# A sandwich block kernel: the chains of the third and fourth batch item are taken with up to two steps in a slot

## The chip, the cores and the metric

The kernel runs on one core of a Trainium2 chip. The metric is the device time of one execution in microseconds (us); lower is better. Each kernel is run several times and the median is given, and one further execution is taken with the hardware profiler on. Engine names in the profile: PE is TensorE (matmuls), PEld its weight loads, DVE is VectorE, ACT is ScalarE, POOL is GpSimd, SP is SyncE, which in this kernel only issues DMAs.

## The reference

The input x has 16 batch items of 512 tokens with 128 features. Two layers, each with a layernorm before it, a layernorm on its output and a residual, are applied:

```
u  = layernorm(x)
Bu = u @ B_w.T                        # 64 states
h  = causal convolution of Bu with exp(t * log(eig))   # by FFT, real part
y  = h @ C_w.T + D * u
x  = x + layernorm(y)

n  = layernorm(x)
p  = softmax(n @ w_router) * softmax(n @ w_gating / 0.1)   # 8 experts
cw = p / (sum(p) + 1e-9)
f  = sum over experts e of cw[e] * ((silu(n @ w_gate[e]) * (n @ w_up[e])) @ w_down[e])
x  = x + layernorm(f)
```

Every expert (128 to 512 to 128) is computed for every token, so the matmuls of the experts are nearly all of the work.

## The kernel before

**Blocks and slots.** A block b is one batch item: 512 tokens, held as 128 features x 512 tokens for the matmuls. The main loop (`for n in range(total + LAG)`, line 804) runs over slots: a slot n is one quarter (128 of 512 hidden units) of one expert of one block, so a block has 32 slots and the loop 512. In a slot `up(n)` issues six matmuls of 128x512 (gate g and up projection uu, each as three products of split fp32 parts, line 337 to 339), and `down(n - 4)` three more (d). A weight or activation is split into a high part, rounded to fp32r, and a low part that holds the rest. ScalarE takes silu of g (`sg`, line 563), VectorE multiplies it with uu (`gate`, line 574), ScalarE rounds the product to `hi` (line 579), and VectorE or POOL computes `lo` (line 585). g has two banks of PSUM and uu three, so g(n+2) needs silu(n) done, and uu(n+3) needs the reader of uu(n) done. Every engine takes its instructions in the order in which the program issues them, and so does SP's DMA queue: an instruction that waits holds up all behind it on its engine.

**After an expert.** In the first slot after its last `down` has been issued and two more have passed (slot 32b + 9, then every fourth slot), `combine` multiplies the expert's output by the token weights `cwb` on VectorE (line 600 for the first expert of a block, 605 for others) and POOL adds (line 608). When a block is done, `back(b)` transposes it through DRAM (`ob`, four `sco` writes, one `ot` read, lines 472 to 480), normalises it and stores it.

**Chains.** What a block needs ahead of its experts is a generator, `chain(b)`: `front(b)` (line 345) and `route(b)` (line 407). front: statistics of xt, its layernorm u, u transposed to features, split into uh and ul, the product bu (three matmuls), times a table (v), a running sum (scan, line 380), times the table, the product yp, plus du, a layernorm, the residual x2, a layernorm xn, xn transposed, split into xh and xl. Blocks 0, 1 and 15 are transposed on TensorE; the others go through DRAM in `features`: a transpose within 32x32 squares on VectorE (`blk_u` or `blk_x`, line 324), four writes `scr` (line 327), and one read `ft` (line 332) that waits on SP until the writes have landed. route: logits on TensorE (line 414), eight exponentials on POOL (line 432, 1.64 us each), normalisation on VectorE, then `cwT`, four small writes `scw` (line 453), and four reads `cwb` (line 461) of 512 KB each, which spread the weights of two experts over all partitions; three buffers hold them.

**The planner.** Chains are cut into steps. A generator yields ahead of each step `delay, DVE, ACT, POOL` (and "f" when the step takes the single bank ps_f): how many slots after the step before it may come at the earliest, and what the step is thought to cost each engine. `busy` holds what is issued on the three engines and not worked off at 1.94 us a slot; `take` refuses a step that would go over. For every chain in order of its rank (block number, and b + 0.5 for `back(b)`), `steps(n)` (line 791) takes up to `1 + hurry` steps in slot n, and shortens each delay by `hurry` unless the step takes ps_f:

```
for _ in range(1 + hurry):
    if n >= x[0] and not (own[0] and x[1][3:]) and take(x[1][:3]):
        ...
        x[0], x[1] = n + (y[0] if y[4:] else max(y[0] - hurry, 0)), y[1:]
```

`begin(n, rank, g, hurry=0)` (line 786) enters a chain: block 0's route and block 1's chain at slot 0 with hurry 1, every later chain at slot max(4, 32 b - 67) with hurry 0, so block 2 at slot 4, block 3 at slot 29 and block 4 at slot 61. Block 2's experts begin at slot 64 and block 3's at 96. Two delays are counted from the slot at hand: `max(1, 32 * b - 8 - now[0])` ahead of cwT, and `max(1, 32 * b + 8 * i + 2 - now[0])` ahead of each cwb. Which engine computes lo (`lo_pool[n]`, line 842) follows from `busy` too: POOL when it has less to do than VectorE.

**Early slots.** Through slot 26 the weights of the experts are split as well (`split_w`, line 113): ScalarE and POOL each have one 128x512 operation for it in three slots of four, and SP loads five ahead.

Of the kernel before, what the change touches and what calls it, by code (L numbers as in the profile page):

```python
# [47 lines left out]
def sandwich(ctx, tc, x, a_params, B_w, C_w, Dv, w_router, w_gating, w_gate, w_up, w_down, sines, out):  # L48
# [417 lines left out]
    def back(b, acc):  # L466

        x2 = blocks[b]["x2"]
        yield 2, 0.6, 0, 0
        ob = work(f"ob{b}").rearrange("p (q c i) -> p q c i", q=4, c=NT)  # L470
        order = "p (c q i) -> p q c i" if on_pe(b) else "p (q c i) -> p q c i"
        vec.transpose(ob, acc.rearrange(order, q=4, c=NT))
        scr = dram.tile([4, 32, 4, P], F32, name=f"sco{b}", tag="sco")
        for j in range(4):
            nc.sync.dma_start(
                out=scr[:, :, j].rearrange("q i m -> i q m"),
                in_=ob[32 * j : 32 * j + 32].rearrange("p q c k -> p q (c k)"),
            )
        ot = work(f"ot{b}").rearrange("p (j c k) -> p j c k", j=4, c=NT)
        nc.sync.dma_start(out=ot.rearrange("p j c k -> p (j c k)"), in_=scr.rearrange("q i j m -> (q i) (j m)"))  # L480
        views = [ot[:, :, c] for c in range(NT)]
        rs, nm = yield from ln_coef(views, 6)
        if "x2m" in blocks[b]:
            vec.tensor_tensor(nm, nm, blocks[b]["x2m"], ALU.add)
        jk = x2.rearrange("p c (j k) -> p c j k", j=4)
        yield from ln_add(gp, jk, ot.rearrange("p j c k -> p c j k"), views, views, jk, rs, nm)
        nc.sync.dma_start(out=out[b].rearrange("(c p) d -> p c d", p=P), in_=x2)
# [65 lines left out]
    def up(n, between=lambda: None):  # L553
        b, e, fc = n // 32, n // 4 % 8, n % 4
        B = blocks[b]
        cs = slice(128 * fc, 128 * fc + 128)
        g = ps_g.tile([P, T], F32, name=f"g{n}", tag="g")
        mm3(g, W[0, e], cs, B["xh"], B["xl"], True, True)
        between()
        u = ps_u.tile([P, T], F32, name=f"uu{n}", tag="u")  # L560
        mm3(u, W[1, e], cs, B["xh"], B["xl"], True, True)
        s = hp.tile([P, T], F32, name=f"sg{n}", tag="sg", bufs=2)
        act.activation(s, g, AF.Silu)  # L563
        pend[n] = s, u
# [3 lines left out]
    def gate(n):  # L568
        s, u = pend[n]
        if lo_pool[n]:  # L570
            h = hp.tile([P, T], F32, name=f"hh{n}", tag="hh", bufs=2)
        else:
            h = u
        vec.tensor_tensor(h, s, u, ALU.mult)  # L574
        pend[n] = h

    def split_hi(n):
        hi = hp.tile([P, T], F32R, name=f"hi{n}", tag="hi", bufs=LAG + 1)
        act.copy(hi, pend[n])  # L579
        pend[n] = pend[n], hi  # L580

    def split_lo(n):
        h, hi = pend[n]
        lo = hp.tile([P, T], F32R, name=f"lo{n}", tag="lo", bufs=LAG + 1)
        (gp if lo_pool[n] else vec).tensor_tensor(lo, h, hi.bitcast(F32), ALU.subtract)  # L585
        pend[n] = hi, lo

    def down(n):
        b, e, fc = n // 32, n // 4 % 8, n % 4
        if fc == 0:  # L590
            dps[b, e] = ps_d.tile([P, T], F32, name=f"d{n}", tag="d")
        cs = slice(128 * fc, 128 * fc + 128)
        mm3(dps[b, e], W[2, e], cs, *pend.pop(n), fc == 0, fc == NF - 1)

    def combine(b, e):
        ps = dps.pop((b, e))
        cw = blocks[b]["cwb"][e // 2][:, e % 2]
        if e == 0:
            accs[b] = fe.tile([P, T], F32, name=f"acc{b}", tag="acc")
            vec.tensor_tensor(accs[b], ps, cw, ALU.mult)  # L600
        elif b == NB - 1 and e == E - 1:
            finish(b, accs.pop(b), ps, cw)
        else:
            t = hp.tile([P, T], F32, name=f"ct{b}_{e}", tag="ct", bufs=2)
            vec.tensor_tensor(t, ps, cw, ALU.mult)  # L605
            eng = vec if (b, e) >= (NB - 1, E - 3) else gp
            acc = accs[b]
            add = lambda: eng.tensor_tensor(acc, acc, t, ALU.add)  # L608
            if (b, e) == (NB - 1, E - 2):
                late.append(add)  # L610
            else:
                add()

    def chain(b):
        yield from front(b)
        yield from route(b)
# [4 lines left out]
    def split_next(k):  # L621
        nonlocal nsplit
        for _ in range(k):
            if nsplit < 3 * E:
                split_w(nsplit)
                nsplit += 1
# [151 lines left out]
    def take(need, most=(0.9, 0.8, 2.0)):  # L778

        if any(c and busy[i] + c > SLOT + most[i] for i, c in enumerate(need)):  # L780
            return False
        for i, c in enumerate(need):
            busy[i] += c
        return True

    def begin(n, rank, g, hurry=0, head=None):
        d, *need = head or next(g)
        side.append([n + d, need, g, hurry, rank])
        side.sort(key=lambda x: x[4])

    def steps(n):
        for x in list(side):
            hurry = x[3]
            for _ in range(1 + hurry):
                if n >= x[0] and not (own[0] and x[1][3:]) and take(x[1][:3]):
                    own[0] = own[0] or bool(x[1][3:])
                    y = next(x[2], None)
                    if y is None:
                        side.remove(x)
                        break  # L800
                    x[0], x[1] = n + (y[0] if y[4:] else max(y[0] - hurry, 0)), y[1:]

    own[0] = False
    for n in range(total + LAG):
        b, s = divmod(n, 32)
        now[0] = n
        busy = [max(0.0, t - SLOT) for t in busy]
        if n < total:
            take((0.6, 1.0, 0), (9, 9, 9))
        if 0 <= n - 1 < total:  # L810
            take((0, 0, 1.23) if lo_pool[n - 1] else (0.6, 0, 0), (9, 9, 9))
            split_hi(n - 1)
        if n < total:
            up(n, *[first] * (n == 0))
        if n == 0:
            begin(n, 0, first_route, 1, routed)
            if NB > 1:
                begin(n, 1, chain(1), 1)
        if n == 3:
            act.copy(bT[0], bT32)  # L820
            gp.tensor_tensor(bT[1], bT32, bT[0].bitcast(F32), ALU.subtract)
        for i in range(NB):
            if i > 1 and n == max(4, 32 * i - LEAD):
                begin(n, i, chain(i))
        m = n - LAG
        if 0 <= m < total:
            down(m)
        m = n - LAG - (2 if n < total else n == total)
        if m >= 0 and m % 4 == 3:
            take((0.6, 0, 1.23), (9, 9, 9))  # L830
            combine(m // 32, m // 4 % 8)
            if m % 32 == 31 and m // 32 in accs:
                begin(n, m // 32 + 0.5, back(m // 32, accs.pop(m // 32)))
        if nsplit < 3 * E and n < total and n % 4 < 3:
            take((0, 0.5, 1.23), (9, 9, 9))
            split_next(1)
        if n < total:
            steps(n)
        if 0 <= n - 1 < total:
            split_lo(n - 1)  # L840
        if n < total:
            lo_pool[n] = busy[2] < busy[0] and n < total - 3
            gate(n)
# [27 lines left out]
```

## Time and profile before

| | us |
|---|---|
| median of 3 runs (lowest, highest) | 1145.75 (1145.21, 1145.89) |
| the profiled execution | 1146.53 |
| its span, first to last instruction | 1144.7 |
| TensorE busy | 1121.9 |
| VectorE, ScalarE, POOL busy | 870.9, 710.3, 764.9 |
| DMA, mean over the span | 62 GB/s |

Where TensorE is idle, by stretches of 20 us (20 less its busy time there): 7.2 in 0 to 20, 3.0 in 20 to 40, 0.6 in 40 to 60, 1.5 in 60 to 80, 0.3 in 80 to 100, 0.4 in 120 to 140, 2.8 in 180 to 200, and 2.2 in 1120 to 1140; in all others it is 0. A busy matmul is counted for about 0.39 us while the next one starts 0.229 us after it, so busy time tells only where TensorE waits; how long is read from the starts.

Slot times, as the start of g(n) in the trace: slot 4 at 33.87, 8 at 44.46, 13 at 55.57, 19 at 69.84, 30 at 98.04, 37 at 112.61, 44 at 127.67, 47 at 133.99, 64 at 171.61, 73 at 190.21, 76 at 199.97. An undisturbed slot takes 2.07 us.

### The profile page before, as it was taken

Reading aid. Unit: us, or ns where it says so; the run is one execution under the profiler, and the core shown is the slowest. Engines: PE = TensorE matmul, PEld = TensorE weight load, DVE = VectorE, ACT = ScalarE, POOL = GpSimd, SP = SyncE. Lnnn points to the kernel's source line nnn. Section 1 sums busy time; section 2 is a strip of 40 time slices with the busy share of each in tenths; the row PEclk is TensorE's granted clock in tenths of the full one; section 3 lists DMA queues with packets and bytes.
Section 4 is the critical chain, followed back from the end, with each engine's and each line's share of the span. In section 5 each row is a group of like instructions: output and inputs, shape, how many; then the busy total and the mean of one; then the engine's idle time right before and its main releaser. Section 6 shows DMA issues by size and latency. Waiting matters only on the chain.

```text
span 1144.7 us, 16089 instructions
## 1 busy us (share of the span) xinstructions
PE 1121.9 (98%) x4969; PEld 913.7 (80%) x4969; DVE 870.9 (76%) x2000; ACT 710.3 (62%) x1346; POOL 764.9 (67%) x641
## 2 busy tenths in 40 slices
PE   7999999999999999999999999999999999999997
PEld 4678787888888888888888888888888888888885
DVE  7878777787878778787777878777777877867666
ACT  3775655665666665666666665666666565666563
POOL 1788685775858668595866858677685776748452
PEclk9999999999999999999999999999999999999999
DMA  4140302203131120312202130121302202021120
GB/s 154 65 139 1 121 28 79 70 11 111 37 93 47 53 87 19 111 37 67 74 29 93 35 114 28 54 70 45 102 29 74 74 19 74 29 74 29 32 71 10
DMA packets 65894, 71.23 MB, mean 62 GB/s; under 512 B 8624, under 2 KB 50320, under 8 KB 65808
## 3 DMA queue, kind: packets, MB, share of 16 engines
q1 hardware_dynamic: 65392, 70.04, 19.8%
q8 instruction: 39, 0.64, 0.2%
q14 instruction: 47, 0.39, 0.1%
q10 hardware_dynamic: 416, 0.16, 0.1%
HBM read 54.98 MB, written 15.20 MB: 61 GB/s over the span
## 4 chain that ended last, share of the span: by engine, by line
PE 82%; DVE 2%; DMA 1%; issue 0%; ACT 0%; SPq 0%; DVEq 0%
PE d L337 9%; PE g L337 9%; PE d L338 9%; PE d L339 9%; PE g L338 9%; PE uu L337 9%; PE uu L339 9%; PE g L339 9%; PE uu L338 9%; PE yp L386 1%; PE lg L414 1%; DVE uu L574 1%; DMA cwb<-scw 0%; DVE lo L585 0%; ACT hi L579 0%
## 5 line engine op out<-in xcount | busy, mean ns | idle before, releaser
L579 ACT CAST hi<-uu 128x512 fp32r<-128x512 f32 x334 | 195.9, 587 | 219.7 <-DVE uu L574 200.4
L585 POOL TENSOR_TENSOR lo<-hh,hi 128x512 fp32r<-128x512 f32 x178 | 233.5, 1312 | 147.4 <-ACT hi L579 144.6
L563 ACT ACTIVATE sg<-g 128x512 f32<-128x512 f32 x512 | 306.7, 599 | 22.5 <-PE g L339 16.7
L585 DVE TENSOR_TENSOR lo<-uu,hi 128x512 fp32r<-128x512 f32 x334 | 229.1, 686 | 113.0 <-ACT hi L579 107.0
L574 DVE TENSOR_TENSOR uu<-sg,uu 128x512 f32<-128x512 f32 x334 | 231.2, 692 | 108.6 <-ACT sg L563 102.0
L608 POOL TENSOR_TENSOR acc<-acc,ct 128x512 f32<-128x512 f32 x109 | 145.3, 1333 | 119.2 <-DVE ct L605 107.1
L579 ACT CAST hi<-hh 128x512 fp32r<-128x512 f32 x178 | 110.6, 621 | 163.9 <-DVE hh L574 161.6
L337 PE MATMUL g<-xh,wgh 128*128 128x512 f32 x512 | 205.8, 402 | 2.3 <-ACT sg L563 1.5
L337 PE MATMUL uu<-xh,wuh 128*128 128x512 f32 x512 | 200.3, 391 | 5.7 <-DVE lo L585 5.7
L337 PE MATMUL d<-hi,wdh 128*128 128x512 f32 x512 | 203.5, 397 | 0.0
L338 PE MATMUL d<-hi,wdl 128*128 128x512 f32 x512 | 201.9, 394 | 0.0
L338 PE MATMUL g<-xh,wgl 128*128 128x512 f32 x512 | 201.3, 393 | 0.0
L339 PE MATMUL d<-lo,wdh 128*128 128x512 f32 x512 | 201.0, 393 | 0.0
L339 PE MATMUL g<-xl,wgh 128*128 128x512 f32 x512 | 199.8, 390 | 0.0
L339 PE MATMUL uu<-xl,wuh 128*128 128x512 f32 x512 | 199.6, 390 | 0.0
L338 PE MATMUL uu<-xh,wul 128*128 128x512 f32 x512 | 199.5, 390 | 0.0
L432 POOL TENSOR_TENSOR ez<-bases,ez 128x8 f32<-128x8 f32 x120 | 195.0, 1641 | 0.0
L574 DVE TENSOR_TENSOR hh<-sg,uu 128x512 f32<-128x512 f32 x178 | 120.9, 679 | 14.4 <-ACT sg L563 8.5
L337 PEld LDWEIGHTS uu<-xh,wuh 128*128 128x128 f32 x512 | 96.2, 188 | 29.9 <-DVE lo L585 7.9
L337 PEld LDWEIGHTS g<-xh,wgh 128*128 128x128 f32 x512 | 96.3, 188 | 25.8 <-ACT sg L563 4.6
L339 PEld LDWEIGHTS d<-lo,wdh 128*128 128x128 f32 x512 | 96.9, 189 | 23.4
L339 PEld LDWEIGHTS g<-xl,wgh 128*128 128x128 f32 x512 | 96.4, 188 | 23.2 <-DVE xl L754 0.4
(173 smaller groups left out, 1330.0 us busy)
## 6 DMA issues: line engine op xcount, KB each, us to landing
cwb<-scw SPq DMA_DIRECT2D x64, 512.0 KB
xt<-in_L_attn_u_dram SPq DMA_DIRECT2D x15, 256.0 KB
sco<-ob SPq DMA_DIRECT2D x60, 64.0 KB
ot<-sco SPq DMA_DIRECT2D x15, 256.0 KB
out_dram<-x SPq DMA_DIRECT2D x15, 256.0 KB
scr_u<-blk_u SPq DMA_DIRECT2D x52, 64.0 KB
ft_u<-scr_u SPq DMA_DIRECT2D x13, 256.0 KB
scr_x<-blk_x SPq DMA_DIRECT2D x52, 64.0 KB
```

Source lines behind the costliest of these rows:

```text
L337: pe.matmul(ps, w[0][:, cs], mh, start=first, stop=False)
L338: pe.matmul(ps, w[1][:, cs], mh, start=False, stop=False)
L339: pe.matmul(ps, w[0][:, cs], ml, start=False, stop=last)
L386: pe.matmul(yp[:, c], v[:, P * c : P * c + P], cT, start=True, stop=True)
L414: pe.matmul(lg[:, 2 * c : 2 * c + 2], xT[:, P * c : P * c + P], wrg.rearrange("d g e -> d (g e)"), start=True, stop=True,)
L432: gp.tensor_tensor(ez[:, i], bases.rearrange("p c g e -> p (c g) e")[:, i], ez[:, i], ALU.pow)
L563: act.activation(s, g, AF.Silu)
L574: vec.tensor_tensor(h, s, u, ALU.mult)
L579: act.copy(hi, pend[n])
L585: (gp if lo_pool[n] else vec).tensor_tensor(lo, h, hi.bitcast(F32), ALU.subtract)
L608: add = lambda: eng.tensor_tensor(acc, acc, t, ALU.add)
```

## The change

The two blocks whose number is 2 or 3 (the third and fourth) are begun with hurry 1, as block 1 is:

```diff
         for i in range(NB):
             if i > 1 and n == max(4, 32 * i - LEAD):
-                begin(n, i, chain(i))
+                begin(n, i, chain(i), int(i <= 3))
```

They begin in the same slots as before. In `steps` up to two of their steps may be taken in a slot, as far as `take` allows, and their delays are one slot shorter except ahead of the steps that take ps_f. Nothing that is computed changes, nor how often; the order of instructions on each engine and in SP's queue does, and with `busy` the choice of VectorE or POOL for lo in a number of slots.

## The prediction

> **What bounds the kernel now.** I read four views, in this order: busy time by engine, windows of 20 us, the waits, and the timeline around the places they point at. First the page and two windows (columns: stretch, length, then busy us of PE, PEld, DVE, ACT, POOL, the granted clock, DMA share, GB/s):
>
> ```profile
> PE 1121.9 (98%) x4969; PEld 913.7 (80%) x4969; DVE 870.9 (76%) x2000; ACT 710.3 (62%) x1346; POOL 764.9 (67%) x641
> ```
> ```profile
> 180.00:200.00 20.00, 17.17 (x74) 13.52 (x73) 12.65 (x34) 10.33 (x21) 8.26 (x8) 0.97 0.34 106
> ...
> 220.00:240.00 20.00, 20.00 (x97) 16.69 (x96) 15.76 (x35) 10.53 (x20) 17.10 (x14) 1.00 0.12 40
> ```
>
> TensorE is the bound: nine matmuls fill a slot in 2.07 us, and from 203 us to 1120 us it never waits. No matmul is added or taken away here, so the time can change only where TensorE stands still between 25 and 203 us. The largest such place is in the window of 180 to 200. Who waited (engine and line, for whom; total us, times, longest), and the timeline of TensorE and the DMA queue there:
>
> ```profile
> DVE acc L600 <- DMA cwb<-scw: 6.5, 2, 5.2
> PE uu L337 <- DVE lo L585: 5.7, 5, 2.8
> ```
> ```profile
> 185.89 2.83 SPq L453 DMA_DIRECT2D scw<-cwT  x4
> 188.83 1.83 SPq L475 DMA_DIRECT2D sco<-ob  x4
> 192.12 0.34 SPq L480 DMA_DIRECT2D ot<-sco  x1
> 192.57 0.37 SPq L461 DMA_DIRECT2D cwb<-scw  x1
> ```
> ```profile
> 194.80 0.39 PE L339 MATMUL g<-xl,wgh 128*128 128x512 f32 x1
> 198.03 0.50 PE L337 MATMUL uu<-xh,wuh 128*128 128x512 f32 x1 [2.83 <-DVE lo L585]
> ...
> 200.39 0.63 PE L338 MATMUL g<-xh,wgl 128*128 128x512 f32 x1
> ...
> 202.47 0.39 PE L337 MATMUL d<-hi,wdh 128*128 128x512 f32 x1
> ```
>
> Block 2's expert weights (cwb) are asked for at 192.57, behind another block's output transpose in SP's queue; VectorE, which needs them for the first combine of slot 73, waits until 196.68; the split low parts behind it come late, and TensorE with them. From the matmul at 194.80 to the one at 202.47 are 13 steps, which take 2.98 us at the usual 0.229 us and took 7.67: **4.7 us lost**, 3.0 of them the wait and 1.7 a half clock from 198.98 to 202.39. The other stops in reach are small: 0.8 us at 56, 2.0 us at 70 to 74, 0.4 us at 97, 0.7 us at 127.
>
> **The change, step by step.** Blocks 2 and 3 get hurry 1: two steps per slot, and each delay one slot shorter unless the step takes the bank ps_f. Going through the planner's budgets with both settings gives the slots.
>
> *The wait at 194.80.* Block 2's chain then issues its first cwb at slot 65 (was 71; the line that holds it back says 66, less one). The combine stays in slot 73. Eight slots are 16.5 us; the load took 4.1 us from issue to the end of the wait. So 4.7 us go. Next late there is nothing: ScalarE's silu has 1.6 to 2.0 us to spare before its buffer is wanted in slots 70 to 72 (start of g(n+2) less end of sg(n)). Block 3's cwb moves from slot 100 to 97, where nothing waited: 0.
>
> *Slots 4 to 30.* Block 2's steps move forward: transpose blk_u from slot 11 to 8, uh 18 to 12, bu 21 to 16, scan 24 to 19, du 30 to 22, statistics 31 to 23. Here VectorE, ScalarE and VectorE again form a loop (gate 0.69, hi 0.62, silu 0.60, each in queue order) of 1.95 us against the slot's 2.07, so a delay is made up by only 0.1 us a slot and silu's spare time is 0.5 to 1.0 us up to slot 26. Gains: without blk_u (0.70) in slot 11 the stop at 56 shrinks by 0.4; bu (three matmuls, 0.69) falls into the stop at 70 instead of after it, 0.7; together -1.1. Losses: VectorE now waits in slot 16 for bu itself (v stands behind it in the same slot; lo and gate queue behind v); the scan (1.55 mean, budgeted 0.6) lands in slot 19 next to statistics of block 1; du and four bn_stats (0.69 + 1.1) come in 22 and 23. 3 us more of VectorE in these slots, of which the stop at 70 and the later matmuls cover two thirds: +0.8. POOL: ul, du and v come 5 to 7 slots earlier, and POOL's split of the expert weights (1.29 each, until slot 26) is due four slots later, so it stands behind them at no cost. Sum **-0.3**, ends -1.1 and +1.0.
>
> *Slots 37 to 47, the new jam.* Features go through DRAM for blocks 2 and 3: four scr writes, a wait for their landing on SP, one ft read. Their copy (uh, xh) on ScalarE comes 4 slots after the transpose instead of 6. SP's queue now holds, from slot 37: scw x4, cwb of block 1, scr_x x4 and ft_x of block 2 (slot 38, was 46), sco x4 and ot of block 0, scr_u x4 and ft_u of block 3 (slot 40, was 43), then cwb. Only the load of xt leaves it (to slot 32). Before:
>
> ```profile
> 115.88 2.84 SPq L453 DMA_DIRECT2D scw<-cwT  x4
> 119.96 0.33 SPq L461 DMA_DIRECT2D cwb<-scw  x1
> ...
> 120.90 2.15 SPq L475 DMA_DIRECT2D sco<-ob  x4
> 126.09 0.34 SPq L480 DMA_DIRECT2D ot<-sco  x1
> ...
> 129.15 1.77 SPq L327 DMA_DIRECT2D scr_u<-blk_u  x4
> 132.29 0.34 SPq L332 DMA_DIRECT2D ft_u<-scr_u  x1
> 135.47 1.76 SPq L327 DMA_DIRECT2D scr_x<-blk_x  x4
> ```
>
> From a first write to its read are 3.14 us (129.15 to 132.29); the last DMA packet of that read ends 2.4 us after its issue. So after: cwb 119.96, scr_x 120.4, behind cwb's traffic ft_x at about 124.8 (sco stood in that place and was done at 126.09, with the xt load beside it); sco 125.2, ot 128.4, scr_u 128.8, ft_u 131.95, landed 134.4. ft_x lands at 127.2, just as ScalarE reaches xh (silu(42) ended at 127.6): nothing. But uh of block 3 is in slot 44, where ScalarE arrives near 131.5 (silu(44) ended there): it stands still for about 3 us. Behind it in its queue are hi(44) and silu(45), and g(47) needs the bank that silu(45) frees: landing + 0.5 + 0.5 + 0.6 = 136.0 instead of 133.99. POOL's last exponentials of block 1 are budgeted 0.4 later, which delays scw: **+2.5**. Ends: +1.0 (the wait spread over the queue, xt's 256 KB gone) and +4.2 (each landing at the longest that SP waited, 2.6 us for scr_u and 3.7 for sco).
>
> *Slots 48 to 66.* After that stop silu has no spare time, and block 3 brings v and the scan at 47 and 51, du at 58, bn_stats at 59 and 63; before, spare time was 0.6 to 2.6 us there: **+0.6**, ends 0 and 1.2. ft_x of block 3 (transpose 66, copy 70) needs 0.7 + 3.1 + 2.4 after VectorE gets there, near 4 slots; silu's 2 us cover the rest: 0.
>
> *The clock.* In the trace an idle stretch of 2.83 us brought the clock to 0.5 for 3.41 us, while 1.43 us at 70.3 brought nothing. The Trainium skill (TensorE: Matmul & The Clock Gate, Part 1) lets the clock fall after at least one idle window of about 3.4 us. By the page an idle time of about 2 us at slot 47 costs nothing (sum below); by the row the limit lies between 1.43 and 2.83, and it may cost the same 1.7 us again. I take 0, nearer to 1.43, and keep 1.7.
>
> **Sum:** -4.7 - 0.3 + 2.5 + 0.6 + 0 = -1.9. The profiled execution took 1146.53, span 1144.7 and 1.8 around it; that gives 1144.6. It lies 0.78 above the median of the three runs, 1145.75, so against that I forecast **1143.8**. A measurement of this kernel can tell about 0.2%, 2.3 us, from no change: it is just inside.
>
> **Rivals.**
> - *The full gain.* SP drains faster than I add up, or the wait of ScalarE is covered by silu's spare time, and only the 4.7 and the 0.3 count, less 0.2: 1145.75 - 4.8 = 1141.0. For it: of the 16 us from 115.88 to 131.95 some 5 are waits for landings behind cwb's 512 KB, whose length in the new order no row fixes. Against it: uh in slot 44 is 4 slots behind blk_u, and five groups of transfers stand before it.
> - *The jam takes back more (slower).* One mechanism, ft_u of block 3 landing late in SP's queue with ScalarE blocked on it: at the high end +4.2, then the idle time exceeds 2.83 us and the clock halves, +1.7, and the loop is without spare time after, +1.2: 1145.75 - 4.7 - 0.3 + 7.1 = 1147.9, and with the early slots at their bad end (+1.3) 1149.2. It decides from a jam of 7.3 us in all on (4.7 + 0.3 + 2.3). For it: the longest SP waits; against: none of them occurs together in the trace.
> - *The change doesn't reach the wait:* cwb of block 2 still late. SP would have to be blocked from slot 65 to 71; ahead of it is only the xt load of slot 62, which waits for one POOL add. Then 1145.75 + 2.8 = 1148.6.
>
> **Chances.** Small gain 0.56 (own range 1142.4 to 1146.0; of it 0.14 below 1143.5); full gain 0.27; jam 0.14; wait remains 0.03. Faster by over 0.2%: 0.14 + 0.27 = 0.41; slower: 0.12 of the jam and 0.02 of the last, 0.14; within: 0.45. The range takes in the full gain and the moderate jam: 1140.6 to 1147.4.
>
> **What would show it.** Right: no wait of L600 for cwb near 190 us and clock 1.00 in 180 to 220; ScalarE idle before uh L356 from 131.5 us on, released by a DMA, and TensorE idle there on silu; SP's ft_u at about 132. Wrong: no wait of L356 (then the full gain), a clock below 1.00 near 135 to 140 us or TensorE idle above 3 us there (then slower), or new stops of over 1 us before 100 us.

## The result, and the profile after

| | before | after |
|---|---|---|
| median of four runs, us | 1145.82 | 1153.16 |
| span of the profiled execution, us | 1144.7 | 1151.2 |

The ratio is 1.0061, with a 95% interval of 1.0045 to 1.0077: the change makes the kernel slower by some 7 us. TensorE does the same matmuls; only its stops have changed. The page's first row, and two rows of the list of waits between 25 and 210 us (sum of us, how often, longest):

```profile
PE 1123.1 (98%) x4969; PEld 911.3 (79%) x4969; DVE 868.6 (75%) x2000; ACT 713.3 (62%) x1346; POOL 766.5 (67%) x641
```
```profile
DVE s L275 <- POOL x L301: 5.2, 2, 3.8
ACT uh L356 <- DMA ft_u<-scr_u: 4.7, 1, 4.7
```

The wait for cwb is gone from the list, and these two, which the list before does not have, have come; each is the wait of a step for the step that it reads on another engine or in a DMA queue. For a count by place, take the time from each matmul's start to the next one's, subtract the median of that pair of matmuls in the same run, and add what is left by slots (good to some 0.2 us):

```
us lost     before   after
slots 0-12    2.7     2.7
13-30         3.9     5.8
31-35         0.0     2.7
36-43         0.0     1.9
44-47         0.7     4.5
48-69         0.1     2.6
70-79         4.7     0.0
80-129        0.3     0.1
```

Up to slot 130 that is 7.8 us more (8.0 by the starts of slots 0 and 130); the profiled execution began its slot 0 at 23.65 us instead of 25.26, which gives 1.6 of it back in the span. That part is luck: the instructions up to there are the same in all fourteen traces, and the start lies between 23.5 and 25.5. The two new waits in turn. VectorE in slot 32, where the statistics of x2 wait for POOL's add:

```profile
104.05 0.68 DVE L574 TENSOR_TENSOR uu<-sg,uu 128x512 f32<-128x512 f32 x1
108.49 0.49 DVE L275 BATCH_NORM_STATS2 s<-x 128x6 f32<-128x128 f32 x2 [3.75 <-POOL x L301]
108.89 0.67 DVE L585 TENSOR_TENSOR lo<-uu,hi 128x512 fp32r<-128x512 f32 x1
```

POOL is at that time busy with exponentials of block 1 (four in 6.45 us from 100.77), and the add stands behind them in POOL's queue; lo and gate stand behind the statistics in VectorE's. Then SP's queue and ScalarE around slot 44:

```profile
119.96 2.83 SPq L453 DMA_DIRECT2D scw<-cwT  x4
124.03 0.33 SPq L461 DMA_DIRECT2D cwb<-scw  x1
124.48 2.06 SPq L327 DMA_DIRECT2D scr_x<-blk_x  x4
128.78 0.34 SPq L332 DMA_DIRECT2D ft_x<-scr_x  x1
129.16 1.87 SPq L475 DMA_DIRECT2D sco<-ob  x4
133.63 0.34 SPq L480 DMA_DIRECT2D ot<-sco  x1
134.01 1.87 SPq L327 DMA_DIRECT2D scr_u<-blk_u  x4
137.63 0.34 SPq L332 DMA_DIRECT2D ft_u<-scr_u  x1
```
```profile
134.82 0.60 ACT L563 ACTIVATE sg<-g 128x512 f32<-128x512 f32 x1
140.15 0.62 ACT L356 CAST uh<-ft_u 128x512 fp32r<-128x512 f32 x1 [4.72 <-DMA ft_u<-scr_u]
140.67 0.61 ACT L579 CAST hi<-hh 128x512 fp32r<-128x512 f32 x1
141.19 0.59 ACT L563 ACTIVATE sg<-g 128x512 f32<-128x512 f32 x1
```

This is the jam of the prediction, row for row: scr_x, ft_x, sco, ot, scr_u, ft_u follow each other on SP, each read waits there for its writes, and ScalarE stands still on uh with hi and silu behind it. TensorE stops at the end of that:

```profile
138.81 0.40 PE L339 MATMUL d<-lo,wdh 128*128 128x512 f32 x1
141.83 0.50 PE L337 MATMUL g<-xh,wgh 128*128 128x512 f32 x1 [2.63 <-ACT sg L563]
```

The matmuls after it start 0.43 us apart, at half the clock, until 145.6. And where the wait for cwb was (slot 73 now starts at 202.12 us instead of 190.21), TensorE now runs through: the window of 200 to 220 us, in the columns of the prediction's windows, has TensorE busy for all of its 20.00 us, at a granted clock of 1.00:

```profile
200.00:220.00 20.00, 20.00 (x93) 16.54 (x92) 16.08 (x36) 11.35 (x22) 16.63 (x13) 1.00 0.27 87
```

The same list of waits has four smaller rows on which the other new losses bear:

```profile
PE yp L386 <- POOL v L382: 0.8, 1, 0.8
PE bu L339 <- POOL ul L359: 0.6, 1, 0.6
DVE blk_x L324 <- ACT xn L295: 1.9, 1, 1.9
DVE sm L435 <- POOL ez L432: 1.0, 1, 1.0
```

In the first two, in slots 22 and 16, TensorE itself stands still for a step of block 2 on POOL; before, it waited 0.3 us for v in slot 29 and not for ul. The other two are waits of VectorE: for ScalarE's xn of block 3 in slot 66, and, just before slot 58, for the last exponential of block 2 on POOL (before, this row has 1.2 us, of block 1, where TensorE did not stop).

### The profile page after: what moved, and what is told of

It is laid out like the page before. It is cut to its first block, busy times and chain, and to the rows that moved or that the text cites. A ratio compares the mean times of both kernels' runs of the same rounds, so it can differ in the third digit from the quotient of the medians.

```text
span 1151.2 us, 16097 instructions
## 1 busy us (share of the span) xinstructions
PE 1123.1 (98%) x4969; PEld 911.3 (79%) x4969; DVE 868.6 (75%) x2000; ACT 713.3 (62%) x1346; POOL 766.5 (67%) x641
## 4 chain that ended last, share of the span: by engine, by line
PE 84%; DVE 2%; ACT 1%; issue 1%; POOL 1%; DMA 0%; DVEq 0%; ACTq 0%; POOLq 0%
PE g L337 9%; PE d L337 9%; PE d L338 9%; PE d L339 9%; PE g L338 9%; PE uu L337 9%; PE uu L339 9%; PE g L339 9%; PE uu L338 9%; PE yp L386 1%; PE lg L414 1%; DVE uu L574 0%; POOL ez L432 0%; DVE lo L585 0%; ACT sg L563 0%
## 5 line engine op out<-in xcount | busy, mean ns | idle before, releaser
L339 PEld LDWEIGHTS g<-xl,wgh 128*128 128x128 f32 x512 | 96.3, 188 | 23.1 <-DVE xl L754 0.4
```

The lines of the kernel that those rows point to most:

```text
L339: pe.matmul(ps, w[0][:, cs], ml, start=False, stop=last)
```

## The experiments

Three theories stood against each other. **W**: a shortened delay puts a step into the slot of the step that it waits for on another engine, or too near a transfer, and an in-order engine stands still. **J**: the jam at ft_u of block 3 is the whole loss. **C**: steps drawn forward crowd slots that are already full. Ratios are to the kernel before on the same chip; "lost" is the count by slots from above.

**e1 and e2, one block alone.**

```diff
-                begin(n, i, chain(i), int(i <= 3))
+                begin(n, i, chain(i), int(i == 2))     # e1
+                begin(n, i, chain(i), int(i == 3))     # e2
```

> Only block 2 is hurried. Theory W (steps that now stand in the same slot as the one they read on another engine make in-order engines stand still, in slots 13 to 35 for block 2 and at ft_u of block 3 in slot 44): slots 13 to 35 lose 8.4 us as in the changed kernel (before 3.9), the stop at slot 47 with its half clock is gone, the cwb wait of 4.7 us is gone: 1145.5 to 1148. Rival J (the jam at ft_u of block 3 is the whole loss): 1141 to 1142. Rival C (the mere crowding of steps in slots 37 to 70 costs): above 1149.

> Only block 3 is hurried. Block 2's first cwb then goes out at slot 68, ahead of the output transpose of slot 71. W: the cwb wait of 4.7 us is gone, ft_u of block 3 (slot 40) has no scr_x of block 2 ahead of it and lands about 130, before ScalarE wants it in slot 44, slots 13 to 35 are as before: 1141 to 1143. J and C: block 3's chain alone makes the stop at slot 47: 1146 to 1149.

e1: 1155.48, ratio 1.0076 (1.0061 to 1.0091): W and J missed, and the time lies where C has it, but not for C's reason, since slots 36 to 69 lost only 2.9 us. Slots 13 to 35 lost 8.4 us, as W said, and the stop at slot 47 was gone (slots 44 to 47: 0.75). But slots 80 to 129 lost 8.3, at one place. SP's queue and TensorE of e1 there:

```profile
264.12 2.81 SPq L453 DMA_DIRECT2D scw<-cwT  x4
266.98 1.90 SPq L475 DMA_DIRECT2D sco<-ob  x4
270.33 0.34 SPq L480 DMA_DIRECT2D ot<-sco  x1
270.77 0.37 SPq L461 DMA_DIRECT2D cwb<-scw  x1
```
```profile
276.16 0.79 PE L337 MATMUL uu<-xh,wuh 128*128 128x512 f32 x1 [5.43 <-DVE lo L585]
```

This is the old wait for cwb, one block later. With block 2 alone hurried, the planner puts scw of block 3 into slot 102 and its first cwb into 103 (before, 99 and 100), and that cwb stands behind sco and ot of block 2; the combine that needs it is in slot 105. TensorE stands idle for 5.4 us, and the clock is halved for 6.8 us from 274.65 on.

e2: 1146.37, ratio 0.9996 (0.9985 to 1.0007), 3 us above W's range: the 4.7 us of cwb were gone, but slots 38 to 73 lost 5.4 us, in stops of 1.0 to 1.3 us at 43, 47, 51 and 73 (before, 0.7 in these slots), and slot 19 lost 1.1 more. ScalarE waited 1.5 us for ft_u, so scr_x in SP's queue is only a part of the jam.

**e3 and e4, one step of the change put back each.**

```diff
-        rs, nm = yield from ln_coef(tiles(x2), 1)
+        rs, nm = yield from ln_coef(tiles(x2), 2 if b in (2, 3) else 1)     # e3
-        yield 5, 0, 0, 0                                                    # features
+        yield (8 if name == "u3" else 5), 0, 0, 0                           # e4
```

> The changed kernel with one delay put back: the statistics of x2 stay one slot behind POOL's residual add (block 2: slot 33 for 32). W: VectorE's wait of 3.8 us for POOL and the 2.6 us that TensorE loses in slots 31 to 35 go, and a part of the 1.9 us in slots 36 to 43: 1149.5 to 1150.8. C: it stays above 1152.

> The changed kernel with the copy uh of block 3 three slots later (slot 47 for 44), all else ahead of it as it is. W and J: no ScalarE wait for ft_u, no 2.63 us idle TensorE near 139, no half clock: 4.5 us less, 1148 to 1149.5. C: the stop moves to another place, above 1152.

e3: 1151.43, ratio 1.0044 (1.0029 to 1.0058). Slots 31 to 35 lost 0.7 instead of 2.7; VectorE's longest wait for POOL's x fell from 3.8 to 1.4 us. The median came out just above the range; its runs lie between 1149.96 and 1153.99, and in the profiled one, the fastest, the stop of 2.8 us at slot 47 came without a half clock. e4: 1148.93, ratio 1.0024 (1.0017 to 1.0031), as W and J said: slots 44 to 47 lost 0.0 instead of 4.5, and no wait of uh is left. J alone is out, since the kernel is still slower than before. In this profile the stop of 2.0 us in slot 34 came with a half clock, which it did not in the changed kernel.

**e12, the order in SP's queue.**

```diff
+        if b == 0:
+            yield 3, 0, 0, 0
         scr = dram.tile([4, 32, 4, P], F32, name=f"sco{b}", tag="sco")
```

> The changed kernel with the four sco writes and the ot read of block 0 issued three slots later, behind scr_u and ft_u of block 3 in SP's queue; the copy uh stays in slot 44. If SP's order is what makes ft_u late, it lands some 4.5 us earlier, ScalarE's wait of 4.7 us falls below 1 us, the stop at slot 47 (4.5 us with the half clock) below 1 us: 1149 to 1150. If the transfers themselves are slow, the wait stays above 3 us and the time at 1152 to 1154.

1149.79, ratio 1.0032 (1.0018 to 1.0045). The copy uh stands where it stood; only sco and ot of another block went behind scr_u and ft_u:

```profile
128.99 1.87 SPq L327 DMA_DIRECT2D scr_u<-blk_u  x4
134.01 0.34 SPq L332 DMA_DIRECT2D ft_u<-scr_u  x1
```
```profile
ACT uh L356 <- DMA ft_u<-scr_u: 1.3, 1, 1.3
```

ft_u went out 3.6 us earlier (4.5 were expected), the wait fell from 4.7 to 1.3 us (below 1 was expected) and slots 44 to 47 lost nothing. So most of the delay is SP's order; the wait for the writes themselves did not shrink (5.0 us from first write to read, instead of 3.6). Some of it came back: slots 60 to 65 lost 2.6 instead of 0.5.

**e6, both put back at once** (the edits of e3 and e4 together).

> The changed kernel with both put back, the slot between POOL's add and the statistics of block 2 and the later copy uh of block 3. W: both losses go at once, 2.0 (e3) and 4.5 (e4), and what stays over the kernel before is slots 13 to 23 (+2.4) and 48 to 69 (+2.4) less the cwb wait: ratio 1.000 to 1.002. If the stops only follow each other (one resource that is full): no better than e4, 1.0024.

1147.08, ratio 0.9998 (0.9989 to 1.0008). The time is just below the range. The two losses are separate and add up, and without them the change is worth nothing either way: the 4.7 us gained are used up by slots 13 to 30 (5.8 instead of 3.9), 38 to 43 (1.8 instead of 0.0) and 48 to 69 (2.8 instead of 0.1).

**e8, the early slots.**

```diff
-        yield 1, 0.6, 0, 0                                # ahead of v
+        yield (2 if b == 2 else 1), 0.6, 0, 0
```

> The changed kernel with one delay put back: v of block 2 not in the slot of its product bu, which moves v from slot 16 to 19, the scan to 20 and du to 24. W: TensorE's losses in slots 13 to 23 fall from 5.6 us to about 3.2 as before (VectorE no longer waits for bu behind POOL's ul, and the scan no longer stands beside block 1's statistics in slot 19). C: they stay at 5 or more, only later.

1152.87, ratio 1.0051 (1.0038 to 1.0065). Slots 13 to 23 lost 4.3 and slots 24 to 30 1.6: together 5.9, as much as in the changed kernel (5.8), only later. W's figure (3.2) is missed, and C's (5 or more) too, but for the stretch as a whole nothing is gained. This does not decide between them: the edit moves v, and leaves ul next to bu and POOL's v next to yp, so TensorE still waits for POOL at both places, 0.6 and 1.0 us. For C speaks that VectorE was busy for 21.4 of 27.7 us in slots 13 to 23 of the kernel before and for 24.8 of 31.0 in the changed one, POOL for 23.1 and 26.6: block 1's chain, the splits and now more of block 2's chain meet there. Further on, slots 38 to 43 of e8 lost 5.2 us instead of 1.7, and 44 to 47 only 0.4 instead of 4.5.

**e7, e9, e10 and e11: the parts of "hurry", and its time.**

```diff
-            for _ in range(1 + hurry):
+            for _ in range(1 + (hurry if x[4] < 2 else 0)):                           # e9
-                    x[0], x[1] = n + (... max(y[0] - hurry, 0)), y[1:]
+                    x[0], x[1] = n + (... max(y[0] - (hurry if x[4] < 2 else 0), 0)), y[1:]      # e7
+                    x[0], x[1] = n + (... max(y[0] - hurry, 0 if x[4] < 2 else min(y[0], 1))), y[1:]   # e10
```
```diff
-            hurry = x[3]                      # of the kernel before
+            hurry = 1 if x[4] in (2, 3) and n >= 31 else x[3]     # e11
```

> Blocks 2 and 3 may take two steps in a slot, but their delays are not shortened; block 2's first cwb goes out in slot 67. W: no step stands in the slot of the one that it waits for, uh of block 3 is 5 slots behind its transpose; the cwb wait goes: ratio 0.996 to 0.999. C (two steps in a slot crowd VectorE and POOL): above 1.002.

> The other half of hurry alone: delays of blocks 2 and 3 one slot shorter, but one step in a slot (first cwb of block 2 in slot 66). No step can stand in the slot of the one ahead of it. W (the product of both halves costs): as e7 below the kernel before, ratio 0.995 to 0.999. If shortened delays cost by themselves: above 1.002.

> Both halves, but a delay of 1 is not shortened to 0, so that a step never stands in the slot of one that it waits for across engines; delays of 2 and 5 are shortened (uh of block 3 four slots behind its transpose, slot 48). W: no VectorE wait for POOL's x, for ScalarE's u or xn or for bu; ratio 0.995 to 0.999. C (chains drawn forward crowd the slots): above 1.002.

> Blocks 2 and 3 hurried from slot 31 on alone. Slots 13 to 30 lose what they lose in the kernel before (3.9 us, or up to 6.2 where the stop at slot 19 halves the clock), not the 5.8 of the changed kernel; x and its statistics of block 2 come in slots 36 and 37 or the same one, ft_u of block 3 behind fewer transfers. C for the early slots: ratio 1.000 to 1.003, 2 to 4 us below the changed kernel.

e7: 1144.30, ratio 0.9977 (0.9962 to 0.9993). e9: 1143.14, ratio 0.9973 (0.9963 to 0.9982). Each half alone is faster than the kernel before, and in neither does a step stand in the slot of the one that it waits for: slots 31 to 35 and 44 to 69 together lost 0.5 us in e7 and 0.6 in e9 (before 0.8, changed 9.7). For slots 44 to 69 this speaks against C, since by the planner block 3's steps in e7 are as early as in the changed kernel (bu in slot 47 in both, x in 60 and 62). For slots 13 to 30 neither run is a test: block 2's steps stand there almost where they stood before (du in slot 27 and 30, changed 22). e7 still lost 1.7 us in slot 43, where VectorE waited 2.8 us for cwb of block 1, whose route ended a slot later. e11: 1144.53, ratio 0.9985 (0.9976 to 0.9995), below the expected range: slots 13 to 30 lost 5.7, of it 4.0 in slot 19 with a half clock, against 3.9 in the kernel before and without that clock; slots 20 to 30, where the changed kernel lost 4.2, lost 0.6.

e10: 1153.80, ratio 1.0063 (1.0046 to 1.0080), against W. With no step in the slot of the one that it waits for it is as slow as the changed kernel, most of it from one stop in slot 43, which cost 8.8 us with a part of its half clock:

```profile
DVE acc L600 <- DMA cwb<-scw: 8.7, 1, 8.7
```
```profile
122.01 1.77 SPq L475 DMA_DIRECT2D sco<-ob  x4
125.24 0.34 SPq L480 DMA_DIRECT2D ot<-sco  x1
125.70 3.23 SPq L453 DMA_DIRECT2D scw<-cwT  x4
130.12 0.82 SPq L461 DMA_DIRECT2D cwb<-scw  x2
```

The planner, run through with this edit, ends block 1's route two slots later (slot 39 for 37), because block 2's earlier steps take POOL's and VectorE's budget from it. Then sco and ot stand in front of block 1's cwb. It is the wait that the change was to remove in block 2, one block earlier. So W accounts for the stops that e3, e4 and e12 remove, and not for those of e1 and e10.

**e5, the wait alone.** Block 2 is hurried from slot 66 on, in the last steps of its route.

```diff
-            hurry = x[3]                      # of the kernel before
+            hurry = 1 if x[4] == 2 and n >= 66 else x[3]
```

> The kernel before, with block 2 hurried from slot 66 on alone: the last three steps of its route come in slots 67, 67 and 68, its first cwb in slot 68 for 71, and no other chain moves. W (the one real gain of the change is the cwb wait, and hurrying the rest costs): the wait and the half clock near 195 go, nothing else changes: 4.7 us less than before, ratio 0.996. If the wait hangs on something else than the place of that load: ratio 1.000.

1141.89, ratio 0.9947 (0.9928 to 0.9965): faster than both kernels. SP's queue, and the window of the old wait:

```profile
183.26 2.83 SPq L453 DMA_DIRECT2D scw<-cwT  x4
187.32 0.32 SPq L461 DMA_DIRECT2D cwb<-scw  x1
...
190.23 1.78 SPq L475 DMA_DIRECT2D sco<-ob  x4
```
```profile
180.00:200.00 20.00, 20.00 (x88) 16.36 (x88) 14.43 (x37) 13.69 (x28) 10.02 (x10) 1.00 0.37 110
```

The load of cwb now stands ahead of sco. TensorE has no idle time there, and slots 70 to 79 lost 0.0 of the former 4.7.

## Why the prediction was wrong

**The wait at 194.80: right.** 4.7 us were forecast to go, and 4.7 went; e5 shows that its whole worth is had by moving that one load.

**Slots 31 to 36: left out.** The prediction lists no step there and no cost. Block 2's x on POOL and its statistics on VectorE both come in slot 32, since the delay of 1 between them becomes 0, and POOL had a backlog of exponentials. This step, put at nothing, measured 2.7 us, of which e3 recovers 2.0 with one step moved by one slot. The prediction had treated the same pattern for v behind bu in slot 16, and did not go on through the list for every delay that becomes 0.

**Slots 37 to 47: mechanism right, size too small.** Forecast +2.5, with ft_u landing 6.7 us after the start of slot 44 (134.4 against 127.67); it landed 8.2 after (140.15 against 131.94). The queue began later (scw 4.2 us into slot 37 instead of 3.3), and sco waited 4.5 us from its first issue to ot, where the sum had 3.2. Slots 44 to 47 cost 3.8 more than before: the stop 2.8 and the half clock after it 1.7, less the 0.7 that was lost at 127 before. The stop is near the forecast; the clock term was weighed and set to 0, and its other end, 1.7, is what happened. Whether it comes is partly luck (last section): in e3 the same stop came without it. Slots 36 to 43 cost another 1.9, for which the sum has nothing. Silu came out of slot 35 without spare time, where it had 2.6 us before. In e3 it had none either, and these slots lost 2.1; in e4, where the half clock in slot 34 gave it 1.3 us, they lost 0.7. No run tests this alone.

**Slots 4 to 30: wrong sign.** Forecast -0.3, measured +1.9. The gains at slots 13 and 19 were there (13 to 19 lost 1.6 instead of 2.8), but slots 20 to 23 lost 3.9 instead of 0.4. Two steps failed. The sum puts POOL's ul, du and v at no cost, and has only VectorE wait; but the matmuls bu and yp read ul and v, and TensorE lost 0.8 us in slot 16 and 1.4 in slot 22, where it waited for them. And "the stop at 70 and the later matmuls cover two thirds" of the added VectorE work did not hold: slot 21 lost 0.9, where the part lo stood behind the scan and block 1's statistics, and in e8 the loss only moved along. How the rest divides stays open.

**Slots 48 to 66: too small.** Forecast +0.6, measured +1.6 (2.4 with the stop in slot 69). The forecast's reason, no spare time after the stop at slot 47, is wrong: e4 and e6 lose the same with that stop gone. In the trace the losses stand behind waits of the kind of slot 32: VectorE waits 1.0 us for POOL's last exponential of block 2 (slot 58 lost 0.7), 1.4 for POOL's x of block 3 (65 and 66 lost 0.8), and 1.9 for ScalarE's xn in the slot of its transpose blk_x (69 lost 0.9). e7, in which these steps stand at least a slot apart, loses nothing there; they were not put back one by one.

**The rivals.** The slower one named the jam, the half clock and the missing spare time after it, at 1147.9. The first two came and the third did not, and 14 in 100 was too little for a slower kernel, because the two places with no figure of their own (31 to 36) and with the wrong sign (4 to 30) made up 4.9 us (2.7 and 2.2) of the gap of 9.4.

## What to carry to other kernels

When a queue of prefetch steps is sped up, the cost sits in pairs: list every pair of steps whose distance shrinks, on all engines and in the DMA queue, and cost the follower, TensorE too, as standing still for the backlog of the engine it reads from. Speed up only the piece that was late: the last steps of one route, one to three slots earlier, were worth 4.7 us here, and the rest of the chains drawn forward cost 12 (4.7 that went, and 7.3 by which the kernel became slower all the same). And a chain drawn forward takes budget from the chains beside it: in e1 and e10 the late load came back, larger, in block 3 and block 1, and in e7, smaller, in block 1.

## What the runs showed of the hardware

**The half clock follows from the idle time within fixed windows, not from the length of a stop.** By length alone, the stops of all fourteen traces do not sort (from slot 0 to 1110 us; each half clock lasted 3.4 us or twice that):

```
idle of TensorE, us     half clock with it
1.2 to 1.9              no (all stops of this length)
2.0                     yes in e4, no in the changed kernel and in e12
2.6                     yes in the changed kernel, e5, e9 and e11, no in e2
2.8                     yes in the kernel before, no in e3
5.4 and 7.5             yes, for 6.8 us (e1, e10)
```

The clock records of the traces show why. Every half clock begins a whole number of times 3.413 us after the record's first full clock: 53 times in the kernel before (180.91 us), 38 in the changed one (129.71), 28 in e4 (95.57), 16 in e5 (54.61), 17 in e9 and e11 (58.03), 75 in e1 and 35 in e10. Cut the trace into windows at these multiples and add up TensorE's idle time in each (by the profile's count, in which the ends of matmuls are modelled):

```
idle in one window of 3.41 us             clock in the next window
at most 1.88 (e12; e3 1.84, e2 1.79,
  changed kernel at slot 34 1.63)         stays full
1.97 (e4), 2.10 (e9), 2.32 (e5),
  2.34 (e11), 2.46 (before),
  2.63 (changed kernel at slot 47)        half
3.41 (e1, e10)                            half; the next window, idle for
                                          1.5 and 2.3, is followed by half again
```

So in these traces the limit lies between 1.88 and 1.97 us of idle time in one window, and a stop of 2.0 to 2.8 us halves the clock when enough of it falls into one. The prediction put the limit on the stop itself, between 1.43 and 2.83. The Trainium skill (TensorE: Matmul & The Clock Gate, Part 1) names at least one idle window of about 3.4 us: the length of the window agrees with these records, but the window need not be idle throughout, since 1.97 us of it were enough in e4.

**One add on VectorE took 1.08, 1.30 and 1.74 us** (x of block 1, in the kernel before, the changed one and e5), each time beside work of POOL. In all fourteen traces this add, which reads two operands, ends 0.55 us after the end of the POOL instruction that was under way when it started, whether that had 0.5 or 1.2 us to go; and the 128x512 instruction of POOL that starts during the add takes 1.72 to 1.74 us, where others take 1.29. So each looks as if it had waited for the other to end. The kernel before and e5 have the same instructions up to slot 66, yet slot 19 lost 1.7 us in one profile and 4.0 in the other, half clock included.
